# Attention and quantised convolutions on one core: next image's values projected when their tiles are free, value weights folded behind the first scores, last nine rows in another PSUM bank

## The chip, the cores and the metric

The kernel runs on one core of a Trainium2 chip. The metric is the device time of one execution in microseconds (us). A time below is the median of several executions; "span" is the time from the first to the last instruction in a profiled execution, which is some 2 us shorter than the device time of the same run.

Names: PE is TensorE's matmul, PEld its weight load, DVE is VectorE, ACT ScalarE, POOL GpSimd, SP the engine whose queue does most of the transfers. "L472" is a line of the kernel that the profile in question belongs to, so the same operation has other line numbers in another kernel. The lines of the profile name tiles: `psu` is the projection that the scores need (its copy is `u`), `pss` the scores, `psa` the attention sums, `psv` a value projection and `vo` the value tile it is copied to, `psw` the Winograd products, `psc` a convolution, `ps_b` the fold of the value weights (`wvo_sb`), and `unread` matmuls whose result nobody uses, given only to keep PE at work.

## The reference, cut to what matters

```python
# x: (16, 128, 32, 32) f32: 16 images, 128 channels, 1024 positions; 4 heads
def layer0(x, w_qkv, b_qkv, w_out, b_out):            # attention over the positions
    qkv = einsum('bchw,oc->bohw', x, w_qkv) + b_qkv   # per head: q, k, v of 128 channels
    scores = einsum('bnc,bcm->bnm', q, k) * c ** -0.5
    out = einsum('bnm,bmc->bnc', softmax(scores), v)
    return einsum('bchw,oc->bohw', out, w_out) + b_out + x

def layer1(x, w1, w2, gamma1, beta1, gamma2, beta2):
    out = conv3x3(act_quant(x), weight_quant(w1))     # 4-bit activations and weights
    out = act_quant(batchnorm(out, gamma1, beta1))    # statistics over all 16 images
    out = batchnorm(conv3x3(out, weight_quant(w2)), gamma2, beta2)
    return out + x
```

The batch norm needs statistics over all images, so the second convolution can't start before the last image's first convolution is done.

## The kernel before

The images go through the attention one after the other. A head of an image has eight steps; a step computes the scores of 128 keys against all 1024 queries (`scores`), and one step later the products of their exponentials with the values (`attend`). The weights are folded first: `fold_a` makes one matrix for queries and keys, `fold_b` one for values and output, so an image has one value tile per 128 positions for all heads: eight tiles of 128 x 512. Beside this, the first convolution of the image before runs as Winograd products (`products`). The last image's convolution can't be hidden in this way; it is done directly, in three pieces, at the end (`first_conv`).

The parts that the change touches:

```python
        vp = pool("vo", NCH + 4)                 # 12 value tiles; an image has NCH = 8
        ...
        ps_s = pool("ps_s", 2, space=PSUM)       # scores, 2 x 2 banks
        ps_a = pool("ps_a", 1, space=PSUM)       # attention sums, tags a0 and a1
        ps_m = pool("ps_m", 2, space=PSUM)       # tag "mm": two banks for everything else
        ...
        nc.sync.dma_start(out=wqk_sb[0 : P // 2, 0], in_=wqk[0 : P // 2, 0])
        nc.scalar.dma_start(out=wqk_sb[P // 2 :, 0], in_=wqk[P // 2 :, 0])
        nc.sync.dma_start(out=xt[0][:, ts(0, HALF)], in_=x[0][:, ts(0, HALF)])
        nc.scalar.dma_start(out=xt[0][:, ts(1, HALF)], in_=x[0][:, ts(1, HALF)])
        nc.sync.dma_start(out=wvo_sb[0 : P // 2], in_=wvo[0 : P // 2])
        nc.scalar.dma_start(out=wvo_sb[P // 2 :], in_=wvo[P // 2 :])
        ...
        def project_v(b, j):
            ps = ps_m.tile([P, NH * P], F32, tag="mm", name=f"psv_{b}_{j}")
            nc.tensor.matmul(ps, lhsT=xt[b][:, ts(j, P)],
                             rhs=bt_sb.rearrange("p h o -> p (h o)"), start=True, stop=True)
            vos[b, j] = vp.tile([P, NH * P], F32, tag="vo", name=f"vo_{b}_{j}")
            nc.vector.tensor_copy(vos[b, j], ps)     # waits for a free value tile
        ...
        def products(b, l):                          # Winograd products of image b
            ...
            for k in (0, 2):
                ps = ps_m.tile([P, 2, D, D], F32, tag="mm", name=f"psw_{b}_{l}_{k}")
                with tc.issue_after(scored[0]):
                    ...                              # two matmuls
                nc.scalar.copy(m[:, k : k + 2], ps)
        ...
        warm_up(3)
        fold_a(0)
        for hf in range(NHF):
            project_u(0, hf)                         # needs the first image and fold_a
        fold_b()                                     # needs wvo_sb
        ...
        while step < n_steps or later:
            ...
                scores(g, j)
                ...
                if j in (5, 6) and b + 1 < B:
                    project_v(b + 1, 2 * h + j - 5)  # next image's tiles 0..7, two in each head
```

## Time and profile before

2127.66 us (median of 3 runs, 2127.5 to 2127.8). Here is how the span falls into stages. The bounds are starts of single instructions in the trace: the first projection for head 2 of the first image, the first matmul of the last image's first convolution, the first matmul of the second convolution, and the start of the last addition to the output.

| stage | us | what sets its end |
|---|---|---|
| start | 59.49 | loads, the folds, the first one and a half heads of the first image |
| middle | 1964.60 | PE, but for 14 waits of the Winograd products |
| last image's first convolution | 8.86 | PE, then the statistics chain |
| second convolution and output sums | 84.59 | PE, then VectorE's sums |
| end | 8.16 | the last addition, its store, and the closing instructions |

To read it: the 14 waits in the middle are the only repeated idle time of PE. Each of the others comes once.

### The profile page before, as it was taken

The numbers are of one execution on the slowest core, as the hardware profiler recorded it, in microseconds if no ns is written. First come the engines' busy times: TensorE is split into PE (matmuls) and PEld (weight loads), VectorE is DVE, ScalarE is ACT, GpSimd is POOL, SyncE is SP. The second block draws the span as 40 slices with busy tenths as digits, with TensorE's granted clock in tenths as the row PEclk, the third lists the DMA queues.
The fourth block names the chain that finished last, engine by engine and source line by source line (L and its number), as shares of the span: only waits on it lengthen the run. The fifth ranks groups of instructions, "written<-read, shape, count | busy, mean of one in ns | idle before, by whom it ended". The sixth has DMA issues, their size and how long they took to land.

```text
span 2125.7 us, 14843 instructions
## 1 busy us (share of the span) xinstructions
PE 2086.8 (98%) x5277; PEld 939.7 (44%) x5277; DVE 1459.2 (69%) x2171; ACT 739.4 (35%) x858; POOL 6.9 (0%) x16
## 2 busy tenths in 40 slices
PE   9999999999999999999999999999999999999994
PEld 4444444444444444444444444444444444444542
DVE  4776666767677676667758666676767767666776
ACT  2233333333333333333333333333333333333365
POOL 0000000000000000000000000000000000000000
PEclk9999999999999999999999999999999999999997
DMA  2000000000000000000000000000000000000044
GB/s 61 12 20 0 0 20 0 20 0 10 10 0 20 0 20 0 1 20 0 20 1 20 0 0 20 0 20 0 11 9 0 20 1 10 0 0 10 0 169 160
DMA packets 11057, 36.81 MB, mean 17 GB/s; under 512 B 1504, under 2 KB 1888, under 8 KB 10976
## 3 DMA queue, kind: packets, MB, share of 16 engines
q1 hardware_dynamic: 9808, 33.10, 4.2%
q10 hardware_dynamic: 1168, 2.69, 0.4%
q8 instruction: 43, 0.70, 0.1%
q14 instruction: 38, 0.31, 0.0%
HBM read 19.01 MB, written 16.78 MB: 17 GB/s over the span
## 4 chain that ended last, share of the span: by engine, by line
PE 91%; DVE 7%; ACT 1%; issue 0%; DMA 0%; ACTq 0%; DVEq 0%
PE pss L485 38%; PE psa L509 37%; PE psv L464 5%; PE psu L451 5%; PE psc L273 3%; PE psw L719 1%; DVE rb L568 1%; DVE part L532 1%; DVE av L579 1%; DVE es L520 1%; DVE acc L580 1%; ACT e L498 1%; DVE y L866 1%; PE psa L626 0%; DVE side L559 0%; DVE vo L472 0%
## 5 line engine op out<-in xcount | busy, mean ns | idle before, releaser
L485 PE MATMUL pss<-u,x 128*128 128x512 f32 (+1 forms) x2064 | 964.6, 589 | 0.0
L498 ACT ACTIVATE e<-pss 128x1024 f32<-128x1024 f32 x511 | 523.4, 1024 | 1249.6 <-PE pss L485 1213.4
L509 PE MATMUL psa<-e,vo 128*128 128x512 f32 x2016 | 947.8, 592 | 0.0
L520 DVE TENSOR_TENSOR es<-es,e 128x1024 f32<-128x1024 f32 x378 | 461.2, 1220 | 353.8 <-ACT e L498 352.1
L485 PEld LDWEIGHTS pss<-u,x 128*128 128x128 f32 x2064 | 389.9, 190 | 474.1 <-issue 454.4
L509 PEld LDWEIGHTS psa<-e,vo 128*128 128x128 f32 x2016 | 379.1, 190 | 458.7 <-issue 457.7
L472 DVE COPY vo<-psv 128x512 f32<-128x512 f32 x128 | 88.3, 690 | 212.9 <-PE psv L464 212.9
L451 PE MATMUL psu<-x,at_sb 128*128 128x512 f32 x256 | 130.9, 593 | 0.4 <-DMA x<-in_x_dram 0.4
L464 PE MATMUL psv<-bt_sb,x 128*128 128x512 f32 x256 | 130.2, 592 | 0.0
L532 DVE TRANSPOSE_TENSOR_REDUCE part<-es 128x32 f32<-128x1024 f32 (+1 forms) x66 | 80.6, 1221 | 2.2
L568 DVE STREAM_TRANSPOSE rb<-sums 128x1024 f32<-128x1024 f32 (+1 forms) x66 | 80.0, 1212 | 1.8
L518 DVE TENSOR_TENSOR es<-e,e 128x1024 f32<-128x1024 f32 x63 | 76.7, 1217 | 0.0
L464 PEld LDWEIGHTS psv<-bt_sb,x 128*128 128x128 f32 x256 | 48.6, 190 | 61.2 <-issue 60.8
L451 PEld LDWEIGHTS psu<-x,at_sb 128*128 128x128 f32 x256 | 48.4, 190 | 61.6 <-issue 53.6
L726 ACT COPY wino<-psw 128x512 f32<-128x512 f32 x120 | 65.6, 589 | 24.9 <-PE psw L719 24.9
L710 DVE TENSOR_TENSOR tiles<-rows 128x1024 bf16<-128x1024 bf16 x60 | 72.0, 1220 | 1.1 <-PE psw L719 0.6
L456 DVE TENSOR_SCALAR u<-psu,au_sb 128x512 f32<-128x512 f32 x64 | 47.8, 746 | 32.4 <-PE psu L451 32.4
L273 PE MATMUL psc<-pad,wq 128*128 128x512 bf16 (+3 forms) x333 | 68.0, 365 | 1.1 <-ACT y L284 0.6
L579 DVE TENSOR_TENSOR av<-av,rb 128x1024 f32<-128x1024 f32 x47 | 57.5, 1223 | 1.9
L580 DVE TENSOR_TENSOR acc<-acc,av 128x1024 f32<-128x1024 f32 x47 | 57.3, 1220 | 0.5
L525 ACT COPY av<-psa 128x512 f32<-128x512 f32 x63 | 36.9, 586 | 37.1 <-PE psa L509 37.1
L273 PEld LDWEIGHTS <-wq 128*128 128x128 bf16 x333 | 32.2, 97 | 37.0 <-DVE pad L248 1.0
(121 smaller groups left out, 749.0 us busy)
## 6 DMA issues: line engine op xcount, KB each, us to landing
x_dram<-x SPq DMA_DIRECT2D x16, 512.0 KB, 2.6
res<-x_dram SPq DMA_DIRECT2D x16, 512.0 KB, 9.4
x<-in_x_dram SPq DMA_DIRECT2D x14, 512.0 KB, 3.6
out_dram<-y SPq DMA_DIRECT2D x13, 512.0 KB, 4.1
out_dram<-y SPq DMA_DIRECT2D x5, 256.0 KB, 2.3
raw<-in_cw_dram ACTq DMA_DIRECT2D x2, 576.0 KB, 3.7
x<-in_x_dram ACTq DMA_DIRECT2D x1, 512.0 KB, 3.7
wqk_sb<-in_wqk_dram ACTq DMA_DIRECT2D x1, 385.5 KB, 4.0
```

What stands on the lines that cost most here:

```text
L273: last = nc.tensor.matmul(ps, lhsT=wq[n][:, tap, :], rhs=pads[b % NPAD][:, r + dy : r + dy + rows, dx : dx + W], start=(tap == 0), stop=(t ...
L451: nc.tensor.matmul(ps, lhsT=at_sb[:, h, :], rhs=xt[b][:, ts(hf, HALF)], start=True, stop=True)
L464: nc.tensor.matmul(ps, lhsT=xt[b][:, ts(j, P)], rhs=bt_sb.rearrange("p h o -> p (h o)"), start=True, stop=True,)
L472: nc.vector.tensor_copy(vos[b, j], ps)
L485: last = nc.tensor.matmul(ps[:, ts(m, N // len(parts))], lhsT=xt[b][:, ts(key, P)], rhs=us[g][:, queries], start=True, stop=True,)
L498: exps[:] = [nc.scalar.activation(e, ps, AF.Exp).ins]
L509: nc.tensor.matmul(psa[g][m], lhsT=vos[b, j][:, ts(h, P)], rhs=e[:, ts(m, HALF)], start=(j == 0), stop=(j == NCH - 1),)
L520: added = nc.vector.tensor_tensor(es[g], es[g], es.pop((g, j)), ALU.add)
L532: nc.vector.tensor_reduce(part, total.rearrange("p (k c) -> p k c", c=Q), AX.X, ALU.add, apply_transpose=True,)
L568: nc.vector.transpose(rb, rinv.unsqueeze(2).to_broadcast([P, n, Q]))
L579: nc.vector.tensor_tensor(av, av, rb, ALU.mult)
L580: nc.vector.tensor_tensor(accs[b], accs[b], av, ALU.add)
```

## The change

The intent is to take away three gaps in PE's work without changing any of its matmuls. (1) The next image's value tiles 4 to 7 are projected in head 3 of the present image, when the attention has given value tiles back, instead of in heads 2 and 3 on fixed steps. (2) At the start, both transfer queues bring the left half of the first image first, and the fold of the value weights comes behind the first scores. (3) The third piece of the last image's first convolution takes a bank of the attention sums instead of one of the two that the first two pieces fill.

```diff
-        nc.sync.dma_start(out=xt[0][:, ts(0, HALF)], in_=x[0][:, ts(0, HALF)])
-        nc.scalar.dma_start(out=xt[0][:, ts(1, HALF)], in_=x[0][:, ts(1, HALF)])
+        for hf in range(NHF):
+            for i, queue in enumerate((nc.sync, nc.scalar)):
+                half = (ts(i, P // 2), ts(hf, HALF))
+                queue.dma_start(out=xt[0][half], in_=x[0][half])
 ...
             project_u(0, hf)
-        fold_b()
 ...
         def first_conv(r, rows, group):
+            pool, tag = ((ps_m, "mm"), (ps_m, "mm"), (ps_a, "a1"))[group]
             with tc.issue_after(attended[0]):
-                attended[:] = [conv(ps_m, "mm", B - 1, 0, r, rows, group, quantized[0]).ins]
+                attended[:] = [conv(pool, tag, B - 1, 0, r, rows, group, quantized[0]).ins]
 ...
+        values = {(0, 5): 0, (0, 6): 1, (1, 5): 2, (1, 6): 3}
+        values.update({(3, 2): 4, (3, 5): 5, (3, 6): 6, (3, 7): 7})
 ...
                     scores(g, j)
-                if g == 0:
-                    project_v(0, j)
+                if step == 0:
+                    fold_b()
+                if g == 0 and j > 0:
+                    for k in (0, 1) if j == 1 else (j,):
+                        project_v(0, k)
 ...
-                if j in (5, 6) and b + 1 < B:
-                    project_v(b + 1, 2 * h + j - 5)
+                if (h, j) in values and b + 1 < B:
+                    project_v(b + 1, values[h, j])
```

## The prediction

> **What bounds the kernel now.** I read the page's engine totals and slices first, then the waits of TensorE (PE), then the timeline at the places where those waits fall. The page says that PE is the bound from the first slice to the last but one:
>
> ```profile
> PE 2086.8 (98%) x5277; PEld 939.7 (44%) x5277; DVE 1459.2 (69%) x2171; ACT 739.4 (35%) x858; POOL 6.9 (0%) x16
> ...
> PE   9999999999999999999999999999999999999994
> ```
>
> A change that leaves the matmuls alone can win only PE's idle time, 2125.7 - 2086.8 = 38.9 us, and 29 us of that lie after the last convolution (from about 2096.6 us), where no part of this change works. Some 10 us are left. The list of PE's waits says where most of it is:
>
> ```profile
> PE psw L719 <- DVE vo L472: 6.6, 14, 0.5
> PE unread L401 <- POOL sums L222: 1.1, 1, 1.1
> PE psc L273 <- ACT y L284: 0.6, 1, 0.6
> ...
> PE ps_b L423 <- DMA wvo_sb<-in_wvo_dram: 0.5, 1, 0.5
> PE psu L451 <- DMA x<-in_x_dram: 0.4, 1, 0.4
> ```
>
> Columns: total us, times, longest. Fourteen waits of the Winograd products (psw) for the VectorE copy of a value tile (vo), 0.47 us each, and four single ones. The first of the fourteen, in PE's timeline (start, us):
>
> ```profile
> 223.46 1.02 PE L464 MATMUL psv<-bt_sb,x 128*128 128x512 f32 x2
> ...
> 227.75 1.02 PE L464 MATMUL psv<-bt_sb,x 128*128 128x512 f32 x2
> ...
> 240.62 1.88 PE L485 MATMUL pss<-u,x 128*128 128x512 f32 x4
> 242.97 0.38 PE L719 MATMUL psw<-tiles,wino 128*128 128x256 bf16 x2 [0.47 <-DVE vo L472]
> ```
>
> and in VectorE's (DVE) in the same place:
>
> ```profile
> 241.09 1.23 DVE L580 TENSOR_TENSOR acc<-acc,av 128x1024 f32<-128x1024 f32 x1
> 242.23 0.68 DVE L472 COPY vo<-psv 128x512 f32<-128x512 f32 x1
> ...
> 245.30 0.69 DVE L472 COPY vo<-psv 128x512 f32<-128x512 f32 x1
> ```
>
> The value projections at 223.46 and 227.75 are copied out only at 242.23 and 245.30. The code says why. There are 12 value tiles and an image uses 8, so the next image's tiles 0 to 3 find free ones in heads 0 and 1, but its tiles 4 and 5, projected in steps 5 and 6 of head 2, need the tiles that this image's head 3 still has to read. Their results lie some 18 us in both banks of the two-bank pool "mm", which the products use too. When the tile is free, the copy stands behind the normalisation on a busy VectorE, and the products in head 3 stand behind the copy. Four scores matmuls take 1.72 us (0.43 each), so the next matmul was due at 242.34 and came at 242.97: **each wait costs 0.63 us**, more than the 0.47 shown, because the shown end of a matmul lies 0.16 us after the point where the next could start.
>
> **What the Trainium skill says.** (1) "Perfetto Trace Analysis", Identifying the Most-Contended Engine: matmul busy share is no measure of the distance to the roofline. So I read 98% only as "hardly ever idle" and count lost time from start to start; the trace agrees, as 0.47 us of idle time is 0.63 us lost. (2) The same page, Identifying Performance Opportunities: a gap that repeats on the engine that should be full can mean too little SBUF or PSUM for the next tile. The trace agrees to the letter: 14 equal gaps, once per image, with the two banks held. (3) The same page, Optimizing Tensor Performance: independent matmul groups should rotate through different PSUM banks, so that draining one overlaps the next. The third piece of the last convolution breaks this: it waits 0.55 us for the drain of the first. (4) "DMA: Bandwidth & Descriptors", Issuing engines are not separate DMA queues: transfers of all issuing engines share 16 DMA engines and interleave. So two halves of the image that are in flight together delay each other; the trace of before fits (the half on SP lands 3.6 us after its issue, the half on ACT 4.8).
>
> **The change part by part.** No matmul, copy or byte is added or removed; one more DMA issue on each of two queues is.
>
> *Values.* Tiles 0 to 3 are projected in heads 0 and 1 as before; tile 4 moves to head 3 step 2, tile 5 to step 5, tiles 6 and 7 to steps 6 and 7. Tile k of this image is last read by the attention of head 3, one step after its scores, so old tile 0 is released in step 1, and tiles 1 to 3 in steps 2 to 4: each is free before its successor is projected. Both mm banks are then free when the products start in head 3 (steps 0 and 1). How that goes is seen in head 2, where the same image's first two products stand with no value in a bank:
>
> ```profile
> 201.98 1.88 PE L485 MATMUL pss<-u,x 128*128 128x512 f32 x4
> 203.69 0.60 PE L719 MATMUL psw<-tiles,wino 128*128 128x256 bf16 x4
> 204.13 1.88 PE L509 MATMUL psa<-e,vo 128*128 128x512 f32 x4
> ```
>
> There the products follow at 1.71 us with no idle time. So 14 x 0.63 = **8.9 us** go. They are on PE, which sets the end, so they count in full.
>
> *Start.* PE in the timeline:
>
> ```profile
> 5.06 2.28 PE L451 MATMUL psu<-x,at_sb 128*128 128x512 f32 x4 [0.40 <-DMA x<-in_x_dram]
> 7.84 1.13 PE L423 MATMUL ps_b<-wvo_sb 128*128 128x128 f32 x8 [0.49 <-DMA wvo_sb<-in_wvo_dram]
> 8.80 3.60 PE L485 MATMUL pss<-u,x 128*128 128x512 f32 x8
> ```
>
> psu needs the left half of x and at_sb, which VectorE ended at 4.77. With both queues on the left half first, it lands sooner, and psu should start near 4.85: 0.2 us. The second half of psu started 0.3 us late (6.22 instead of 5.06 + 0.86 = 5.92); with no weights of the value fold ahead in the queues, 0.15 of that may go. After psu the kernel waits 0.49 us for wvo (0.66 start to start). In the new order the scores come first; their left half needs u's left half, ready at 6.96, the right half the ScalarE copy of u that ended at 8.07, about 0.7 us after psu. The left half is 0.86 us of matmuls, which covers that but for 0.1 us; then the fold runs (0.97 us from 7.84 to 8.80) with its weights long landed. That wins about 0.55. Sum: **0.9 us**.
>
> *Last nine rows.*
>
> ```profile
> 2024.09 3.03 PE L273 MATMUL psc<-pad,wq 128*128 128x480 bf16 x18
> 2027.67 1.29 PE L273 MATMUL psc<-pad,wq 128*128 128x288 bf16 x9 [0.55 <-ACT y L284]
> ```
>
> The third piece takes the attention's second accumulator bank, which was read last at about 2018 us. Its rows are quantised by 2026.46, so it can start at the pitch of the pieces before it, 0.71 us earlier (0.55 + 0.16). The batch statistics stand right behind it:
>
> ```profile
> 2028.99 0.47 DVE L283 BATCH_NORM_STATS2 late<-psc 128x6 f32<-128x288 f32 x1 [1.40 <-PE psc L273]
> 2029.49 0.25 DVE L310 BATCH_NORM_AGGREGATE mv<-late 128x2 f32<-128x21 f32 x1
> ```
>
> VectorE idled 1.40 us before it, so it can take the statistics earlier; everything to the second convolution (2032.95) hangs on them: **0.7 us**.
>
> Sum: 8.9 + 0.9 + 0.7 = 10.5 us, and 2127.66 - 10.5 = **2117.2 us**.
>
> **The rivals.** (a) *A new wait takes the place of the old.* The value tile 4 comes in step 2 of head 3, just behind the products, when VectorE is at its fullest: busy 13.49 of the 14 us from 236 to 250. If its copy is late, the projections of steps 3 and 4 lack a bank. For it: two banks only, and the instruction order is made beforehand, from estimates. Against it: VectorE's work in head 3 is the same as before, only later by steps; the projection of step 4 comes some 8 us after tile 4; scores have their own banks, four e tiles of slack. If it happens in each image at 0.3 to 0.6 us, 4 to 8 us come back: 2121 to 2125. I give it 12%. (b) *VectorE becomes the bound.* At 69% over the span and idle 2.5 to 3.3 us a step in the later steps of a head, it has room for a copy of 0.69 us in steps 5 to 7; even tile 7 in the last step delays the draining of the accumulators only if idle time is used up. 3%, and worth less than 5 us. (c) *The two small parts are hidden.* The image's second half, now in two pieces behind the first, may land as late as before, and the start wins only 0.3; the tail may win nothing if the statistics wait for something else: 2118.3 together. 20%. (d) *The gap in the products is not the bank alone:* the products are told to issue behind the scores, so a part of the 0.63 could stay. Head 2's products speak against it. 5%.
>
> **Range and chances.** The fall can hardly be larger than the idle time before the tail in start-to-start terms, 11.5 us or so: 2116. Half of (a) gives 2121. Eight in ten: 2115.9 to 2120.6. 2% is 42.6 us, four times what can be won, and no mechanism that I see loses that much: faster by over 2% 0.004, within 2% 0.99, slower 0.006.
>
> **What would show it.** In the profile of after: the line of psw waiting for vo gone from PE's waits (if another fourteen-fold wait stands there, rival a); images spaced 0.63 us closer than before (125.98 us between the gaps that end at 242.97 and 368.95); value copies within 2 us of their matmuls; scores before the fold at the start, with the fold waiting for nothing; the third piece of the convolution without a gap, and PE busy time unchanged near 2086.8. I am wrong if idle time on PE in the middle stays over 2 us, or if the time is above 2121.

## More of the kernel before

TensorE's clock isn't full at the start of a kernel. The moment at which the full clock was granted is in the clock records of the packed trace: 5.09 us after the first instruction in the profile of before, 6.08 in that of after.

## The result, and the profile after

The changed kernel took 2117.64 us (median of 4 runs, 2117.47 to 2117.70), against 2127.73 us (2127.50 to 2127.95) for the kernel before in the same rounds. The ratio is 0.9952, 95% interval 0.9935 to 0.997: within 2%.

By stages, from the profiles of the two:

| stage | before | after | won | predicted |
|---|---|---|---|---|
| start | 59.49 | 59.20 | 0.29 | 0.9 |
| middle | 1964.60 | 1955.75 | 8.85 | 8.9 |
| last image's first convolution | 8.86 | 8.24 | 0.62 | 0.7 |
| second convolution and sums | 84.59 | 84.58 | 0.01 | 0 |
| end | 8.16 | 8.05 | 0.11 | 0 |
| span | 2125.70 | 2115.82 | 9.88 | 10.5 |

The engine totals of the page after:

```profile
PE 2084.8 (99%) x5277; PEld 941.1 (44%) x5277; DVE 1455.0 (69%) x2171; ACT 736.0 (35%) x858; POOL 6.8 (0%) x16
```

The counts of PE's and VectorE's instructions are those of before: only the order and places changed. PE's busy time fell by 2.0 us without a matmul less. A matmul that is followed by a gap is shown 0.16 us longer than its pitch to the next, as the prediction itself had read, so fourteen gaps less are 14 x 0.16 = 2.2 us of shown work less.

PE's waits after (total us, times, longest):

```profile
PE unread L403 <- POOL sums L222: 1.1, 1, 1.1
PE psc L273 <- DVE pad L248: 0.6, 1, 0.6
PE psu L453 <- DVE at_sb L419: 0.2, 1, 0.2
```

That is the whole list. The line of fourteen waits is gone and nothing has come in its place. PE's timeline in head 3 of the first image, where the products come, and VectorE's copies of tiles 4 and 5 (start us, us, instruction):

```profile
237.33 0.60 PE L720 MATMUL psw<-tiles,wino 128*128 128x256 bf16 x4
237.77 1.88 PE L511 MATMUL psa<-e,vo 128*128 128x512 f32 x4
239.49 1.88 PE L487 MATMUL pss<-u,x 128*128 128x512 f32 x4
241.20 1.02 PE L466 MATMUL psv<-bt_sb,x 128*128 128x512 f32 x2
```

```profile
244.81 0.69 DVE L474 COPY vo<-psv 128x512 f32<-128x512 f32 x1
...
255.14 0.69 DVE L474 COPY vo<-psv 128x512 f32<-128x512 f32 x1 [2.82 <-PE psv L466]
```

The products run as one block of four, and the projection of tile 4 follows them at the usual pitch. Its copy comes 3.6 us later: it stood behind other work of a busy VectorE. That bank wasn't asked for again in this time, and the next projections (245.49 and 249.78, for the next head) found one. The copy of tile 5 is released by its own matmul, with VectorE idle before it.

The start after, on PE:

```profile
4.82 2.59 PE L453 MATMUL psu<-x,at_sb 128*128 128x512 f32 x4 [0.17 <-DVE at_sb L419]
7.40 1.13 PE L487 MATMUL pss<-u,x 128*128 128x512 f32 x2
8.56 1.16 PE L425 MATMUL ps_b<-wvo_sb 128*128 128x128 f32 x8
```

The first projection starts 0.24 us sooner than before, but takes 2.59 us instead of 2.28. That is the clock and not the kernel: its first matmul, before the full clock, is shown with 1.22 us here and with 0.68 in before, and with 1.22 also in more_tiles, which has the old start and got the full clock at 7.08 us. The order that the compiler made put the fold between the two halves of the first scores. There it starts just behind its weights, whose last part landed at 8.52 us in this trace; PE was free 0.2 us sooner (7.40 + 1.13 - 0.16 = 8.37).

The last image's convolution, on PE and on VectorE:

```profile
2014.95 4.16 PE L273 MATMUL psc<-pad,wq 128*128 128x480 bf16 x27
2018.94 3.61 PE L755 MATMUL unread<-wq,wq 128*128 128x512 bf16 x16
```

```profile
2019.14 0.47 DVE L283 BATCH_NORM_STATS2 late<-psc 128x6 f32<-128x288 f32 x1 [0.69 <-PE psc L273]
2019.64 0.25 DVE L310 BATCH_NORM_AGGREGATE mv<-late 128x2 f32<-128x21 f32 x1
```

All 27 matmuls of the three pieces are one block now, and VectorE waited 0.69 us for the third piece instead of 1.40.

### The profile page after: what moved, and what is told of

Its sections match the earlier page's. It is cut to its first block, busy times and chain, and to the rows that moved or that the text cites. A ratio compares the mean times of both kernels' runs of the same rounds, so it can differ in the third digit from the quotient of the medians. Undisturbed runs are those within 1.5% of the kernel's fastest.

```text
span 2115.8 us, 14862 instructions
## 1 busy us (share of the span) xinstructions
PE 2084.8 (99%) x5277; PEld 941.1 (44%) x5277; DVE 1455.0 (69%) x2171; ACT 736.0 (35%) x858; POOL 6.8 (0%) x16
## 4 chain that ended last, share of the span: by engine, by line
PE 98%; DVE 1%; ACT 0%; issue 0%; DVEq 0%; POOL 0%; POOLq 0%
PE pss L487 42%; PE psa L511 41%; PE psu L453 5%; PE psv L466 5%; PE psc L273 3%; PE psw L720 1%; DVE y L875 1%; PE psa L628 1%; ACT y L874 0%; PE unread L403 0%; PE ps_a L417 0%; DVE es L620 0%; PE ps_b L425 0%; PE psr L552 0%; DVEq L1061 0%
```

## The experiments

Twelve kernels ran, four at a time on one chip beside the kernel before. All gave correct results. The theory was the prediction's: the fourteen waits are the two banks of "mm" held by values that have no tile. The main rivals were a new wait in the old one's place, a gap that isn't the bank's alone, and small parts that are hidden. The stages of all twelve, and the first profile of the changed kernel (us):

| kernel | start | middle | first conv | second conv, sums | end | time | ratio to before |
|---|---|---|---|---|---|---|---|
| after | 59.20 | 1955.75 | 8.24 | 84.58 | 8.05 | 2117.64 | 0.9952 |
| values_only | 60.81 | 1955.75 | 8.86 | 84.58 | 9.54 | 2120.23 | 0.9963 |
| more_tiles | 59.70 | 1955.75 | 8.86 | 84.58 | 9.52 | 2120.17 | 0.9963 |
| one_bank | 59.33 | 1955.82 | 8.24 | 84.57 | 8.07 | 2117.82 | 0.9953 |
| tail_only | 59.61 | 1964.63 | 8.24 | 84.57 | 8.19 | 2127.84 | 1.0001 |
| after_again | 59.65 | 1955.75 | 8.24 | 84.57 | 8.05 | 2118.57 | 0.9957 |
| xhalves_only | 59.81 | 1964.79 | 8.86 | 84.59 | 8.06 | 2128.52 | 1.0004 |
| no_halves | 58.87 | 1955.75 | 8.24 | 84.57 | 9.56 | 2118.78 | 0.9962 |
| fold_behind | 61.29 | 1955.75 | 8.24 | 84.58 | 8.06 | 2117.93 | 0.9953 |
| plus_one | 61.30 | 1955.75 | 8.24 | 84.57 | 9.42 | 2120.07 | 0.9962 |
| trim | 59.07 | 1955.75 | 8.24 | 84.57 | 8.19 | 2117.49 | 0.9950 |
| trim_pool | 58.81 | 1955.75 | 8.24 | 90.93 | 7.58 | 2122.85 | 0.9976 |
| values_undone | 59.17 | 1964.80 | 8.24 | 84.57 | 8.06 | 2127.34 | 0.9998 |

The kernel before ran at 2127.74, 2127.83 and 2127.76 us on the three chips; one of its seven executions on the first took 4830.75 us and is not counted. The start of a kernel varies by some tenths between runs, sometimes by 2 us; the middle repeats to 0.01 us with the new value steps, and to 0.2 us with the waits in it. So stages tell more than times here.

**values_only: the new value steps alone, in the kernel before**

```diff
+        values = {(0, 5): 0, (0, 6): 1, (1, 5): 2, (1, 6): 3}
+        values.update({(3, 2): 4, (3, 5): 5, (3, 6): 6, (3, 7): 7})
 ...
-                if j in (5, 6) and b + 1 < B:
-                    project_v(b + 1, 2 * h + j - 5)
+                if (h, j) in values and b + 1 < B:
+                    project_v(b + 1, values[h, j])
```

> Kernel before with nothing but the new steps of the value projections. Theory (value results held both banks of the pool that the products need): the fourteen waits of the products go and no other takes their place; 14 x 0.633 = 8.86 us less than before, so about 2118.9 us, with the single waits at the start (0.40 and 0.49) and before the third convolution piece (0.55) still there. Rival (the waits went because the new start shifted the phase of the engines, or because only all three parts together free the banks): some or all of the fourteen waits stay, 2121 to 2127.7 us.

The middle fell by 8.85 us, all of it. The time fell by only 7.5 us, to 2120.23 (2120.17 to 2121.34), because the end of the kernel was 1.4 us longer, where the edit changes nothing. That is taken up with plus_one.

**more_tiles: the old steps, two value tiles more**

```diff
-        vp = pool("vo", NCH + 4)
+        vp = pool("vo", NCH + 6)
-        avp = pool("av", 2)
+        avp = pool("av", 1)
```

The second line only makes room, by taking one of the two buffers of the attention's output (`av`): fourteen value tiles and two of those didn't fit into SBUF.

> Kernel before with its old projection steps, but with 14 value tiles instead of 12 (one buffer of the tile av taken away to make room). Theory (the results waited in PSUM because no value tile was free): tiles 4 and 5 are copied out at once in head 2, both banks are free when the products come, the fourteen waits go: about 2118.9 us, as with the moved steps. Rival (the copy is late because VectorE is full in head 3, or the steps themselves matter): the waits stay near 0.63 us each, 2127.7 us; or the single av buffer costs something of its own, seen as new waits on av.

With a tile free for each, the values of the old steps are copied as soon as they are made. VectorE's timeline in head 2 of the first image, where before the two results stayed in the banks until 242.23 and 245.30 us:

```profile
224.72 0.69 DVE L472 COPY vo<-psv 128x512 f32<-128x512 f32 x1 [2.87 <-PE psv L464]
...
229.01 0.69 DVE L472 COPY vo<-psv 128x512 f32<-128x512 f32 x1 [2.47 <-PE psv L464]
```

The middle is 1955.75 us, to the hundredth the same as with the new steps. So it is the missing tile, and not the step, that made the waits, and no part of the 0.63 us of each was due to anything else: the rival of a gap that isn't the bank's alone has fallen.

**one_bank: one of the two values back in head 2**

```diff
-        values.update({(3, 2): 4, (3, 5): 5, (3, 6): 6, (3, 7): 7})
+        values.update({(2, 6): 4, (3, 5): 5, (3, 6): 6, (3, 7): 7})
```

> Changed kernel, but value tile 4 projected in step 6 of head 2, where no value tile is free, so that one of the two banks is held into head 3 and the other is free. If only the holding of both banks made PE wait: no wait or nearly none, 2117.6 to 2118.5 us. If every held bank costs its share: about half of the old loss, 14 x 0.3 = 4.4 us more than the changed kernel, 2122 us. If the products stop as soon as one bank is held: the full 8.9 us come back, 2126.5 us.

PE and VectorE in the first image:

```profile
226.73 1.02 PE L466 MATMUL psv<-bt_sb,x 128*128 128x512 f32 x2
...
234.45 0.38 PE L720 MATMUL psw<-tiles,wino 128*128 128x256 bf16 x2
234.67 1.88 PE L511 MATMUL psa<-e,vo 128*128 128x512 f32 x4
236.39 0.38 PE L720 MATMUL psw<-tiles,wino 128*128 128x256 bf16 x2
```

```profile
242.33 0.68 DVE L474 COPY vo<-psv 128x512 f32<-128x512 f32 x1
```

Tile 4 was made at 226.73 and copied at 242.33: it held one bank for 15.6 us. The products had the other alone, so they came in pairs with four attention or scores matmuls between them, instead of in fours. This cost 0.07 us in the whole middle: a bank is emptied in less time than four such matmuls take.

**values_undone: both back in head 2, everything else of the change kept**

```diff
-        values.update({(3, 2): 4, (3, 5): 5, (3, 6): 6, (3, 7): 7})
+        values.update({(2, 5): 4, (2, 6): 5, (3, 5): 6, (3, 6): 7})
```

> The changed kernel with the value tiles back in their old steps (4 and 5 in head 2), so that both banks are held again. With the one-bank run a series of none, one and two banks held: by the theory two banks bring the whole 8.9 us back, all fourteen waits of 0.63 us, 2126.5 us; with the rival (the new start or the new bank of the last rows had a part in the middle) less, 2118 to 2124 us.

```profile
PE psw L720 <- DVE vo L474: 6.6, 14, 0.5
```

The fourteen waits are back, and the middle is 1964.80. None, one and two banks held thus give 1955.75, 1955.82 and 1964.80 us: the first costs nothing to speak of, the second 9.0.

**tail_only: the bank of the third piece alone, in the kernel before**

```diff
+            pool, tag = ((ps_m, "mm"), (ps_m, "mm"), (ps_a, "a1"))[group]
-                attended[:] = [conv(ps_m, "mm", B - 1, 0, r, rows, group, quantized[0]).ins]
+                attended[:] = [conv(pool, tag, B - 1, 0, r, rows, group, quantized[0]).ins]
```

> Kernel before with nothing but the last nine rows of the first convolution in the other PSUM bank. Theory (they waited for the drain of the first piece, and the statistics hung on them): the wait of 0.55 us goes, the statistics of the third piece and all after them come 0.71 us earlier, 0.6 to 0.7 us at the end, about 2127.0 us. Rival (the statistics or ScalarE's square root wait for something else): the piece starts earlier, the second convolution does not, 2127.7 us.

The stage went from 8.86 to 8.24 us, as in the whole change. The time (2127.84, 2127.05 to 2129.18) doesn't show it: 0.6 us is less than the spread of the runs. On time alone this part is inconclusive, on the stage it is not.

**xhalves_only: the four pieces of the first image alone, in the kernel before**

```diff
-        nc.sync.dma_start(out=xt[0][:, ts(0, HALF)], in_=x[0][:, ts(0, HALF)])
-        nc.scalar.dma_start(out=xt[0][:, ts(1, HALF)], in_=x[0][:, ts(1, HALF)])
+        for hf in range(NHF):
+            for i, queue in enumerate((nc.sync, nc.scalar)):
+                half = (ts(i, P // 2), ts(hf, HALF))
+                queue.dma_start(out=xt[0][half], in_=x[0][half])
```

> Kernel before with nothing but the image's halves in two pieces each. Theory (the two more issues, 0.6 us each, put the value weights off by some 0.7 us, from a landing at 7.75 to 8.5 us, and the fold of the value weights, which stands ahead of the first scores in this order, waits for them): the halves alone are no gain but a loss of 0.6 to 0.7 us, 2128.4 us. Rival (the earlier image wins at the start, as the prediction had it): 0.3 us gained, 2127.4 us.

The start was 59.81 us, not below the 59.49 and 59.61 of the two profiles with the old start in which the clock was granted at nearly the same moment (5.1 and 5.5 us after the first instruction; here 5.3). PE waited 0.96 us for the value weights:

```profile
8.16 1.13 PE L425 MATMUL ps_b<-wvo_sb 128*128 128x128 f32 x8 [0.96 <-DMA wvo_sb<-in_wvo_dram]
```

The extra issue on each queue comes ahead of the value weights, so these were issued at 2.61 and 2.88 us, 0.65 us later than before (1.96 and 2.23); the changed kernel's profile has the same. But the wait itself proves little: it was 0.49 us in before and 0.84 in tail_only, which loads the image in whole halves. The time (2128.03 to 2129.49, against 2127.50 to 2128.68 for the kernel before) is inconclusive: the medians differ by the 0.7 us that was expected, the ranges overlap, and the stage shows 0.2 to 0.3.

**no_halves: the whole change, but for the four pieces**

The edit is the one above the other way round, in the changed kernel.

> The changed kernel with the image loaded in whole halves as before. Theory (after the change the fold waits for the value weights that the two more issues put off): weights land at 7.75 us, the fold follows the first half of the scores without waiting, 0.2 to 0.5 us gained over the changed kernel, 2117.2 us. Rival: the image's left half comes later, 0.2 us lost, 2117.8 us.

```profile
4.88 2.31 PE L451 MATMUL psu<-x,at_sb 128*128 128x512 f32 x4 [0.23 <-DVE au_sb L418]
7.18 1.12 PE L485 MATMUL pss<-u,x 128*128 128x512 f32 x2
8.23 1.16 PE L423 MATMUL ps_b<-wvo_sb 128*128 128x128 f32 x8
```

With whole halves the projection starts only 0.06 us later than with the pieces, and the scores and the fold come 0.22 and 0.33 us sooner. The start is 58.87 us, 0.3 us below that of the changed kernel, though the full clock also came 0.5 us sooner in this run. The value weights did not land at 7.75 us, as expected, but at 8.19, and the fold waited for them here too. The end is again 1.5 us longer, and the time (2118.78, 2118.26 to 2121.5) shows no gain over after_again.

**fold_behind: the fold held behind both halves of the first scores**

```diff
                 if step == 0:
-                    fold_b()
+                    with tc.issue_after(scored[0]):
+                        fold_b()
```

> The changed kernel with the fold held behind both halves of the first scores (the order made at compile time had put it between them). Theory (between the halves it waits 0.2 us for the weights that land at 8.5 us): the fold starts near 9.1 us without a wait, 0.2 us gained, 2117.4 us. Rival (the second half of the scores waits as long for ScalarE's half of u): no change, 2117.6 us.

Its profile fell into a run with another hindrance, so it tells nothing of the order: the clock, granted at 4.2 us, was taken back from 7.6 to 11.0, and before that PE had stood idle for 1.4 us, waiting for the second half of the image. The profile's windows view, in the stretch in question (the last three columns are the granted clock, the share of the DMA engines and GB/s):

```profile
7.60:11.00 3.40, 3.40 (x5) 1.30 (x4) 0.00 (x0) 0.69 (x1) 0.00 (x0) 0.50 0.78 181
```

The median time, 2117.93 (2117.09 to 2119.71), is no better than the changed kernel's. Inconclusive.

**after_again: the changed kernel once more, to learn the spread**

> The changed kernel once more, for the same chip and hour as the three runs beside it: 2117.6 us. So far the moment at which TensorE's granted clock went to full differed from profile to profile (5.1, 6.1, 7.0, 7.1, 5.5, 9.6 us after the first instruction). Theory (that moment belongs to the run, not to the kernel): it differs again from the 6.1 us of the first profile of this kernel. Rival (the earlier start of the first projection moves it): again 6.1 us.

2118.57 us (2117.64 to 2119.31) in a later session, against 2117.64 at first; its start was 59.65 instead of 59.20, with a wait of 0.5 us for the second half of the image that the first profile doesn't have. So the same kernel moves by a microsecond, and nothing smaller can be read from times of this many runs. The full clock came at 6.48 us instead of 6.08: that moment belongs to the run.

**plus_one: one tiny VectorE instruction more**

The kernels values_only, more_tiles and no_halves have an end that is 1.4 to 1.5 us longer, although they don't touch it, and their traces have 2629 records of VectorE and its queue; those of all other kernels so far had 2614, 2615 or 2628. To test whether the count does it, the changed kernel was given one instruction twice, some 2000 us before the end:

```diff
             nc.vector.tensor_scalar(be[:, n : n + 1], beta, mult, None, ALU.mult)
+            if n == 1:
+                nc.vector.tensor_scalar(be[:, n : n + 1], beta, mult, None, ALU.mult)
```

> The changed kernel with one 128x1 VectorE instruction given twice, far from the end (a constant of the second normalisation). In three kernels (the values alone, the 14 tiles, the whole halves) the last store landed 6.8 us after its issue instead of 5.4, and in each the instruction queue had a packet of 901 ns beside it; their traces have 2629 VectorE records, those of the others 2614, 2615 or 2628. Theory (one more instruction moves the end of VectorE's program over a border, and its fetch gets in the way of the last store): 2629 records, the 901 ns packet, 1.4 us more than the changed kernel, 2119.0 to 2119.5 us. Rival (a coincidence): no such packet, 2117.6 to 2118.5 us.

The end went from 8.05 to 9.42 us. The stores' time from issue to landing, first in the changed kernel, then with the instruction added:

```profile
DMA to landing us min/median/max: 1.7/3.8/5.4
```

```profile
DMA to landing us min/median/max: 1.7/3.8/6.8
```

And the queue of instruction transfers from the last sums to the end of each (packets, MB, share of 16 engines):

```profile
q14 instruction: 2, 0.02, 0.5%
```

```profile
q14 instruction: 3, 0.02, 1.0%
```

One instruction more, one packet of instructions more at the very end (it took 901 ns), and the last store lands 1.4 us later.

**trim: no_halves with one VectorE instruction less**

```diff
-            nc.vector.tensor_scalar(be[:, n : n + 1], beta, mult, None, ALU.mult)
+            if n == 1:
+                nc.scalar.copy(be[:, n : n + 1], beta)
+            else:
+                nc.vector.tensor_scalar(be[:, n : n + 1], beta, mult, None, ALU.mult)
```

> The changed kernel with the image in whole halves as before, and one 128x1 VectorE instruction given to ScalarE. By the fetch theory: 2628 VectorE records, the last store lands in 5.4 us again, and the 0.3 to 0.8 us that the whole halves won at the start show in the time: 2117.2 us, the lowest so far. By the rival: 6.8 us and 2118.7 us as without the trim.

2628 records, two instruction packets, the last store back at 5.4 us, the end at 8.19. So the longer end of no_halves came from the count, not from what it does. The time is 2117.49 (2117.07 to 2117.84), ratio 0.9950 with an interval of 0.9936 to 0.9963: the lowest median of all, but not told apart from the change.

**trim_pool: four images' last sums on GpSimd**

The idea was to shorten VectorE's chain of sums at the end, the longest stretch in which PE is idle.

```diff
+                pooled = b in (3, 6, 9, 12)
-                if b == 0 and hi <= N // 2:
+                if pooled or b == 0 and hi <= N // 2:
                     nc.vector.tensor_scalar(y, y, scale2, bias2, ALU.mult, ALU.add)
 ...
-                nc.vector.tensor_tensor(y, y, x1[b][:, lo:hi], ALU.add)
+                adder = nc.gpsimd if pooled else nc.vector
+                adder.tensor_tensor(y, y, x1[b][:, lo:hi], ALU.add)
```

> The same as trim, and in the last stage four of the sixteen images (3, 6, 9, 12) have their normalisation on VectorE instead of ScalarE and their residual sum on GpSimd instead of VectorE. After the last convolution both ScalarE and VectorE are full for 19 us (18 activations, 20 sums of up to 1.14 us apart), and GpSimd is idle. Theory (these two set the end): VectorE loses 4 x 1.14 and gains 4 x 0.6 us, 2.1 us less, ScalarE 4.1 us less, so about 2 us won against trim, 2115 us. Rival (GpSimd's sums are long, or slow VectorE down beside them, or the stores set the end): no gain or a loss, 2117 to 2120 us.

It lost 5.4 us against trim. From the groups of the last 33 us (busy us, mean ns, then the idle time before):

```profile
L878 DVE TENSOR_TENSOR y<-y,res 128x1024 f32<-128x1024 f32 (+2 forms) x16 | 20.7, 1351 | 0.0
L878 POOL TENSOR_TENSOR y<-y,res 128x1024 f32<-128x1024 f32 x4 | 13.8, 3462 | 36.3 <-DMA out_dram<-y 31.7 <-DVE y L874 4.6
```

VectorE does sixteen sums instead of twenty, and needs 20.7 us for them where trim needed 18.6 for all twenty. Single sums beside one of GpSimd's took 3.36 us instead of 1.21, and one normalisation 2.84 instead of 0.80. What GpSimd takes over, VectorE loses again while the two run together.

## Why the prediction was right or wrong

It said 2117.2 us, within 2%; 2117.64 was measured, inside the range. The values are 8.9 of its 10.5 us, so the total could be near although the start was wrong. By its steps:

- *Values, 8.9 us:* right, 8.85, or 0.632 us for each of the 14. The cause is shown twice over: by taking the waits away with more tiles and the old steps (more_tiles), and by bringing them back with nothing else changed (values_undone). Its way of counting from start to start, 0.63 us for a wait shown as 0.47, was needed: the shown 6.6 us would have been 2.2 too few. Images stand 0.62 us closer: products at 237.33 and 362.69 us are 125.36 apart instead of 125.98.
- *Start, 0.9 us:* wrong in size, 0.3. Of its terms, the fold behind the first scores held, and two others failed, for the second half of the image and for the value weights. Compare only profiles in which the full clock was granted 5.1 to 5.6 us after the first instruction. With the fold before the scores and whole halves the start was 59.49 and 59.61 (before, tail_only), with the fold behind and whole halves 58.87 and 58.81 (no_halves, trim_pool): 0.7 us won, against 0.55 predicted. (trim, with the clock at 4.4, had 59.07, so a single profile is good to some 0.3 us.)
  The term for the left half, "With both queues on the left half first, it lands sooner, and psu should start near 4.85: 0.2 us", about held, but for another reason: the left half had landed at 4.59 to 4.86 us in the seven profiles with pieces and at 4.24 to 5.20 in the seven with whole halves, so it comes more evenly rather than sooner. The projection started at 4.79 to 4.95 against 4.82 to 5.34, 0.16 us sooner in the mean. The first step that failed is "0.15 of that may go", for the second half: it landed later, at 5.97 to 7.39 us against 5.11 to 6.51, 0.7 us in the mean, and in three of the seven profiles with pieces PE waited 0.5 to 1.4 us for it.
  The second step that failed is "with its weights long landed": they landed at 8.52, and the fold, which the compiler had put between the halves of the scores, started at 8.56. In no_halves they landed at 8.19 and the fold started at 8.23; this 0.33 us is the whole difference between the two starts. At most a part of it can be laid to the two more issues ahead of the weights. They put off the issue of the weights by 0.65 us, but in all profiles with pieces they landed at 8.07 to 8.55, with whole halves at 7.75 to 8.40, 0.3 us later in the mean.
  In the old order the start with pieces was 0.26 us longer at an equal clock (59.81 against the mean of 59.49 and 59.61), in a single profile. In the new order the difference, 58.81 to 59.07 in three profiles with whole halves and 59.17 to 61.30 in five with pieces and the fold as in the change, can't be put down to the pieces alone, because in all five the full clock also came later (6.1 to 10.5 us against 4.4 to 5.6). So no profile shows a gain from the pieces; whether and how much they cost is open.
- *Last nine rows, 0.7 us:* right, 0.62. The gap of the third piece went and the statistics came 0.71 us sooner, as worked out; VectorE's shorter wait, 1.40 less 0.69, gives the same. Some 0.09 us went again just ahead of the second convolution, where PE waited 0.63 instead of 0.54 us for the pads. It is so in every kernel with the new bank. Why was not found out.
- *Rival (a), a new wait on a bank in head 3:* didn't come. The sign that the prediction named for it, copies within 2 us, failed all the same: tile 4's took 3.6. The sign was badly chosen. A late copy costs only if its bank is wanted meanwhile, and one_bank shows a bank held for 15.6 us at 0.07 us in all.
- *Rival (b), VectorE as the bound:* didn't come; VectorE is idle 2.82 us before tile 5's copy.
- *Rival (c), small parts hidden:* half right, for the start, whose size of 0.3 us it names, and by the mechanism that it names: the second half of the image landed no sooner in pieces. (Its sum is off: 2127.66 - 8.9 - 0.3 is 2118.5, not 2118.3.)
- *Rival (d), a gap that isn't the bank's alone:* excluded by more_tiles.
- *PE busy time near 2086.8:* it fell to 2084.8, which the prediction could have worked out from its own 0.16 us per gap.

Not foreseen at all were changes at the end of the kernel. The 0.11 us won there go with the pieces of the first image: the end is 8.05 to 8.07 us in six profiles with them and 8.16 to 8.19 in three without (those with 1.4 us more and trim_pool apart); why, no run shows. And three of the experiments lost 1.4 us there. This second thing didn't hit the change itself, whose count of VectorE records happened to be 2628, one below the count at which it appears. Without plus_one and trim, values_only would have looked as if the two small parts together won 2.6 us.

## What to carry to other kernels

A result that lies in a PSUM bank because the tile it is to be copied to isn't free yet blocks everybody who shares the bank; look for the projection's start and the copy's start, and if they lie many microseconds apart, move the projection to where the tile is free (or add a tile, if SBUF has room). One of two banks held was harmless here, the second cost all. Cut a kernel's profile into stages before you compare times: parts of half a microsecond could be read in stages and not in times, and an unrelated 1.4 us at the end would have been booked on the wrong edit.

## What the Trainium skill lacked or had wrong

- "Runtime: NRT & Kernel Launch", Instruction fetch mechanics, says that the sequencer fetches instructions through its own DMA queue, block by block, and that crossing a block's border is mostly hidden. In kind this agrees with the instruction queue in these traces. Not hidden was the one that falls to the very end: one VectorE record more (2629 instead of 2628), one packet of 901 ns more, and the last store landed 6.8 instead of 5.4 us after its issue, in four kernels of four. Whether and how this packet holds up the store, no run shows; only that the two came together each time.
- "TensorE: Matmul & The Clock Gate", What's actually happening: its window of 3413 ns agrees with the half-speed stretch of 3.41 us in fold_behind. It gives the moment of the transition as varying by 500 ns either way; here the full clock came between 4.2 and 10.5 us after the first instruction, in kernels whose first instructions are nearly the same, and once it was taken back again. (The page also calls that moment run-variable, which these runs bear out.)
- "DMA: Bandwidth & Descriptors", which the prediction cites for transfers that share the engines, was right as far as it was used. What I missed when I used it is the issue itself: 0.48 to 0.87 us per issue on a queue at the start, so that splitting a transfer in two also puts off the issue of everything behind it, here by 0.65 us; the landing of the value weights moved by 0.3 us in the mean.
- The slow sums beside GpSimd in trim_pool are no gap of the skill: it has pages on these two engines, and I had not used them.
